# A planner that counts a pause between dependent VectorE instructions, with its due dates searched anew, in a one-core attention and scan kernel

## The chip, the cores and the metric

The kernel runs on one core of a Trainium2 chip. The metric is the device time of one execution in microseconds (us), as the median of several runs. The engines are named as the profile names them: PE is TensorE (PEld its weight loads), DVE is VectorE, ACT is ScalarE, POOL is GpSimd, SP is SyncE, which issues the DMAs.

## What is computed

All in fp32, for 4096 rows of x and 3202 rows of context, both 512 wide, with 8 heads of 64:

```python
x = layernorm(builder_state, g1, beta1); base_n = layernorm(base_state, g1, beta1)
q = heads(x, Wq, bq); k = heads(base_n, Wk, bk); v = heads(base_n, Wv, bv)
attn = softmax(einsum('bhqd,bhkd->bhqk', q, k) / sqrt(64))
x = builder_state + (attn @ v).reshape(...) @ W_o.T + b_o
U = (layernorm(x, g2, beta2) @ W_in.T + b_in) @ Bmat
def step(s, u_t):                      # 4096 steps over the rows, 64 states, from zero
    s = silu(s @ A.T) + u_t
    return s, s
out = x + states @ Cmat + (program_probs.mean(1) @ W_prog.T + b_prog)
```

## The kernel before

**The work and its tiles.** A first plan prepares K and V. The main plan, with which this case deals, runs over 64 *units*. A unit is a block Q of 512 queries (8 of them), a pair hp of heads (4) and a half of 256 queries (2); in the first seven blocks unit i has Q = i div 8, hp = (i div 2) mod 4, half = i mod 2. A unit goes through 13 steps c over the keys. In step c PE computes `scores` (L1131, 16 quarter-array matmuls of 64x64 weights into one of two PSUM score banks, ring "s"), ACT the exponential `weights` (L1209, tile p), PE the `product` with V (L1267, into the PSUM pair po0 and po1, ring "o", of which there is one), and DVE adds the weights up over the steps (`add`, L1217, each add taking the result of the one before it: tile acc). At the last step the product also takes in the keys that are left over (L1255).

**The end of a unit.** `output` (ACT, L1317) copies po0 out and `join` (DVE, L1321) adds po1 to the copy. Only then may the next unit's product 0 write the pair. `rest` (DVE, L1202) adds the left-over keys' weights to acc, `fold` (DVE, L1224) adds acc's halves, `swap` (ACT, L1236) copies its partition halves across, `gather` (DVE, L1241) adds that copy, `sums` (PE, L1295) adds over the partitions, `den` (ACT, L1339) takes the sums out, `inverse` (DVE, L1344) and `scale` divide the output by them. `sums` needs both slots of the PSUM ring "m". For every second unit these hold first the sample from which the exponent's shift comes: `sample` (PE, L1151), `maximum` (DVE, L1165), `spread` (PE, L1173), `base` (DVE, L1186 to L1187), and `extra` (ACT, L1193), whose reading frees the slots.

**What runs beside it.** For each block Q the plan also makes the next block's queries and finishes a block before it: `outs` (PE, L391, tiles pax and pay, full-array matmuls through `by_sevenths`, with its reads on DVE at L1664 and `so` at L1646), the row's statistics (DVE L1402, POOL L1406 to L1408), its scaling (ACT, L1414), the flip by 32x32 blocks (DVE, L468), `mod` (POOL, L1710), and the SP transfers. Scans of the 64 states run beside the last units: chain a (PE L1919, ACT, DVE L1954) and chain b; behind the last unit stands a chain l of 20 dependent steps (its rows are normalized into xh_yl, L2105, and turned on PE, L332), then its products (L1993) and outputs.

**What sets the order.** Each engine's order is decided ahead of time by the class `Plan`. A piece has an engine, a cost in ns, the pieces that it comes after, a due date, and ring slots that it takes and gives. `Plan.order` runs a simulated clock: an engine that is free takes, of the pieces that are ready and whose slots are free, the one with the earliest due date. The table `SHIFT` moves the due date of all pieces of one name by a number of STEPs of 2150 ns. A successor on another engine becomes ready `LATE` after the piece's simulated end (150 ns after DVE, 110 after ACT, 250 after PE); a successor on the same engine became ready at the simulated end itself. `OVER` lets the next instruction of DVE start 80 ns ahead of the end of the one before, if it does not depend on it. PE pays 200 and 280 ns for going between quarter-array and full-array matmuls. The order that comes out is the program; on the chip each engine runs its list strictly in that order and waits on semaphores. So costs and dates of the planner cost no time themselves: only the order counts.

```python
heapq.heappush(events, (free[e], -1, p["at"], p))                    # L195: engine free
heapq.heappush(events, (now + cost, 0, p["at"], p))                  # L196: same engine's successors
heapq.heappush(events, (now + cost + self.LATE[e], 1, p["at"], p))   # L197: other engines' successors
```

Of the kernel before, what the change touches and what calls it, by code (L numbers as in the profile page):

```python
# [75 lines left out]
class Plan:  # L76
# [8 lines left out]
    OVER = {"DVE": 80, "ACT": 100}  # L85
    ENTER, LEAVE = 200, 280
# [6 lines left out]
        "row.store": -0.5, "fold": 17, "rows.outs": 8.25, "heads": -12, "spread": 1.75, "query.flip": -11,  # L93
        "states": -4.5, "inverse": 14.75, "extra": 10, "scale": -51.75, "rest": 11, "row.mod": -20,
        "joined0": -10.25, "b": 1, "add.l": -23, "l.stats": -34.75, "last": -4.5, "base": -34.75,
        "inverse.l": -35, "rows.inputs": 5, "maximum": -13.5, "fall": -19, "query.stats": -10, "den": 4.5,
        "row.scaled": 16, "l.h": -11, "row.stats": -21.25, "rows.turn": 11, "query.scaled": 7.5, "l.mod": 7.5,
        "close": -10, "swap": 5.75, "products": -8, "gather.l": -8, "l.ys": -10, "fall.l": -2, "weights": -3.5,
        "rows.s": 2, "l.x1": 1, "l.kept": 8, "tq": 20, "l.store": -2, "row.move3": 9, "l.from": -5,
        "l.copy": -12, "l.states": -8, "l.turn": -4, "row.flip": 3.5, "swap.l": -18, "l.near": 4,  # L100
        "differ": -0.25, "row.load": 12, "add": -6, "rest.l": -8, "den.l": 11.5, "query.factors": 16,
        "sevenths": -6, "l.z": -2, "gather": 1, "scale.l": -0.5, "outs": 1, "output": -12, "query.move3": 3,
        "number": 0.25, "l.inputs": -4, "q": -12, "sums": -4, "row.move2": 10, "row.move1": -0.25,
        "query.move0": -0.5, "stored1": -12, "counted": 1, "to": 12, "sums.l": 9, "row.kept": 8, "so": 11.75,
        "stored0": 2, "l.scaled": -0.25, "row.move0": 4, "rise": -1, "join": -12, "sample": 2.5,
        "l.idle": -0.25, "risen": -0.5, "c2": 0.5, "yb": 2, "query.load": 8,
# [23 lines left out]
    def order(self):  # L130
# [29 lines left out]
        while len(out) < len(pieces):  # L160
            for e in self.LATE:
# [15 lines left out]
                p = best[1]  # L177
# [18 lines left out]
                heapq.heappush(events, (now + cost, 0, p["at"], p))  # L196
# [23 lines left out]
def xattn_ssm_kernel(  # L220
# [1206 lines left out]
    def queries(plan, Q, d):  # L1427
# [4 lines left out]
        for half in range(2):  # L1432
# [171 lines left out]
    def project_by_sevenths(plan, Q, d, index):  # L1604
# [16 lines left out]
        for half in range(2):  # L1621
            for t in range(2):
                k = kss[half][t]
                first = (*kss[half][0], "load")
                plan.add((*k, "load"), "SP", 800, partial(load, half, t),
                         [first] if t else [from_(d - 6 * STEP)], d - 6 * STEP + 2 * half + t, [] if t else ["x"])
                plan.add((*k, "row"), "POOL", 1270, partial(row, half, t),
                         [(*k, "load"), from_(d - 2 * STEP)], d - STEP)
# [134 lines left out]
    def project(plan, Q, halves, d, index):  # L1763

        for half in halves:
# [41 lines left out]
            for t in range(2):  # L1807
                plan.add((*ks[t], "load"), "SP", 800, partial(load, t),
# [727 lines left out]
    with tc.manual_schedule():  # L2536
# [8 lines left out]
            Plan.OVER,  # L2545
        )
# [109 lines left out]
```

## Time and profile before

| | us |
|---|---|
| median of 3 runs (lowest, highest) | 1921.72 (1920.82, 1922.46) |
| the profiled execution | 1921.14 |
| its span in the trace | 1919.4 |
| PE busy | 1892.6 (99%) |
| PEld busy | 1375.6 (72%) |
| DVE busy | 1557.7 (81%) |
| ACT busy | 1174.9 (61%) |
| POOL busy | 253.5 (13%) |

The mean granted TensorE clock was 0.996 of full speed. A row of the timeline gives the start of an instruction in us from the start of the span, how long it took, its engine and line, the tiles written and read, its size, how many like it stand one behind the other (xN), and in brackets how long the engine was idle before it and whose result came last. Matmuls overlap, so the time of a set of 16 is longer than the distance to the next set. In group rows and waits the last numbers are the busy or waiting time, the count, and the mean or longest.

### The profile page before, as it was taken

To read this page: it belongs to the slowest core of one execution; us is meant where nothing else is said; L and a number is where in the kernel's file an instruction comes from. 1 tells how busy PE (TensorE), PEld (TensorE's weight loads), DVE (VectorE), ACT (ScalarE), POOL (GpSimd) and SP (SyncE) were. 2 spreads that over 40 slices of the span, in tenths; PEclk is the share of its full clock that TensorE was granted. 3 is DMA by queue.
4 is the path that set the end of the run, shared out by engine and by line. 5 is a ranking of instruction groups with operands and counts; after the bars stand their busy time and mean duration, and the time that the engine had idled before them with its cause. 6 is when DMAs were issued, how large, how long until landed. Compare 5 with 4: busy or idle time off the path is not lost.

```text
span 1919.4 us, 68812 instructions
## 1 busy us (share of the span) xinstructions
PE 1892.6 (99%) x29632; PEld 1375.6 (72%) x29632; DVE 1557.7 (81%) x2133; ACT 1174.9 (61%) x1675; POOL 253.5 (13%) x386
## 2 busy tenths in 40 slices
PE   9999999999999999999999999999999999999997
PEld 5887677777677767776777777776777677777664
DVE  6642799788979898798978897989879897989675
ACT  3242677575756576657757575657665775756642
POOL 6120300012001210021001200021002100120114
PEclk9999999999999999999999999999999999999998
DMA  8654233133323342323413332334232431545475
GB/s 253 164 150 123 58 102 89 45 104 91 101 63 106 91 114 82 94 70 108 109 42 108 85 106 65 104 93 112 83 91 64 117 107 42 174 119 165 139 205 189
DMA packets 260769, 207.55 MB, mean 108 GB/s; under 512 B 94633, under 2 KB 233897, under 8 KB 260461
## 3 DMA queue, kind: packets, MB, share of 16 engines
q1 hardware_dynamic: 256440, 196.48, 35.7%
q10 hardware_dynamic: 4020, 6.62, 1.2%
q8 instruction: 235, 3.85, 0.8%
q14 instruction: 74, 0.60, 0.1%
HBM read 156.32 MB, written 29.88 MB: 97 GB/s over the span
## 4 chain that ended last, share of the span: by engine, by line


## 5 line engine op out<-in xcount | busy, mean ns | idle before, releaser
L1209 ACT ACTIVATE p<-s,shifts 128x1024 f32<-128x1024 f32 (+1 forms) x832 | 891.9, 1081 | 448.5 <-PE s L1131 422.5
L1217 DVE TENSOR_TENSOR acc<-p,acc 128x1024 f32<-128x1024 f32 (+1 forms) x704 | 841.4, 1195 | 111.2 <-ACT p L1209 81.7
L1131 PE MATMUL s<-q,k 64*64 64x256 f32 x12800 | 859.6, 377 | 3.8 <-ACT p L1209 3.7
L1267 PE MATMUL po<-p,v 64*64 64x256 f32 x12800 | 860.3, 376 | 2.0 <-DVE o L1321 2.0
L1131 PEld LDWEIGHTS s<-q,k 64*64 64x64 f32 x12800 | 501.4, 133 | 211.4 <-ACT p L1209 23.1
L1267 PEld LDWEIGHTS po<-p,v 64*64 64x64 f32 x12800 | 505.3, 133 | 180.3 <-DVE o L1321 6.0
L1619 POOL TENSOR_TENSOR xr<-xr,rowb 128x512 f32<-128x512 f32 x28 | 35.7, 1274 | 850.5 <-DVE acc L1217 739.1
L1344 DVE RECIPROCAL rd<-rd 128x256 f32<-128x256 f32 (+1 forms) x64 | 110.0, 1718 | 6.4 <-ACT rd L1339 6.4
L1217 DVE TENSOR_TENSOR acc<-p,p 128x1024 f32<-128x1024 f32 x64 | 78.3, 1224 | 21.0 <-ACT p L1209 21.0
L1710 POOL TENSOR_TENSOR xr<-x,modb 128x512 f32<-128x512 f32 x28 | 40.9, 1470 | 309.1 <-DVE x L1664 174.9
L1236 ACT COPY swap<-acc 64x256 f32<-64x256 f32 x126 | 50.9, 404 | 18.1 <-DVE acc L1224 15.4
L1241 DVE TENSOR_TENSOR acc<-swap,acc 64x256 f32<-64x256 f32 x126 | 52.3, 415 | 6.7 <-ACT swap L1236 5.1
L1202 DVE TENSOR_TENSOR acc<-x,acc 2x256 f32<-2x256 f32 x128 | 54.9, 429 | 1.5
L1556 ACT ACTIVATE q<-qx,bias 128x256 f32<-128x256 f32 x42 | 17.6, 470 | 56.9 <-PE qx L391 56.9
L569 DVE TENSOR_TENSOR ks<-pky,ks 128x512 f32<-128x512 f32 x15 | 10.4, 692 | 43.6 <-PE pky L391 28.7
L1224 DVE TENSOR_TENSOR acc<-acc 128x512 f32<-128x512 f32 x63 | 43.2, 686 | 0.8
L563 ACT ACTIVATE ks<-pkx,bias 128x256 f32<-128x256 f32 x40 | 16.8, 470 | 44.1 <-PE pkx L391 32.6
L1321 DVE TENSOR_TENSOR o<-po,o 128x256 f32<-128x256 f32 x64 | 26.9, 420 | 11.4 <-ACT o L1317 11.0
L1193 ACT ACTIVATE x<-sm,shifts 128x256 f32<-128x256 f32 x64 | 26.8, 472 | 14.7 <-DVE shifts L1187 14.1
L1406 POOL TENSOR_SCALAR rstd_x<-mv_x 128x1 f32<-128x1 f32 x28 | 12.2, 434 | 175.7 <-DVE mv_x L1403 174.0
L1165 DVE TENSOR_REDUCE m<-sm 128x1 f32<-128x256 f32 x64 | 24.0, 417 | 12.0 <-PE sm L1151 12.0
L1339 ACT ACTIVATE rd<-pd 128x128 f32<-128x128 f32 x126 | 33.2, 271 | 0.4 <-PE pd L1295 0.4
(307 smaller groups left out, 1762.9 us busy)
## 6 DMA issues: line engine op xcount, KB each, us to landing
k<-kd SPq DMA_DIRECT2D x432, 128.0 KB, 2.3
v<-vd SPq DMA_DIRECT2D x432, 128.0 KB, 2.3
xn<-x SPq DMA_DIRECT2D x448, 32.0 KB, 1.9
xr<-in_x_dram SPq DMA_DIRECT2D x30, 256.0 KB, 3.6
x1d<-xr SPq DMA_DIRECT2D x30, 256.0 KB, 2.1
x<-in_x_dram SPq DMA_DIRECT2D x28, 256.0 KB, 3.3
cx<-in_ctx_dram SPq DMA_DIRECT2D x25, 256.0 KB, 4.6
kd<-ks SPq DMA_DIRECT2D x20, 256.0 KB, 2.3
```

Of the source, the lines that this page charges most:

```text
L1131: nc.tensor.matmul(s[k0 : k0 + HD, a, b, :], kts[(*w["at"][:2], c)][r, b * CK + k0 : b * CK + k0 + HD], q[r], start=True, stop=True, skip_ ...
L1202: made = nc.vector.tensor_tensor(to[r], t[r], to[r], ALU.add)
L1209: nc.scalar.activation(t[:, :, :nb, :], w["ps"][c][:, :, :nb, :], AF.Exp, bias=w["shift"])
L1217: return nc.vector.tensor_tensor(w["acc"][:, :, :nb, :], t[:, :, :nb, :], before[:, :, :nb, :], ALU.add)
L1224: return nc.vector.tensor_tensor(acc[:, :, 0, :], acc[:, :, 0, :], acc[:, :, 1, :], ALU.add)
L1236: nc.scalar.copy(w["swap"][r], of[(1 - k) * HD : (2 - k) * HD])
L1241: made = nc.vector.tensor_tensor(of[r], w["swap"][r], of[r], ALU.add)
L1267: nc.tensor.matmul(w["po"][k][a * HD : (a + 1) * HD, :QU], vts[Q, hp, c][r, b, a * HD : (a + 1) * HD], t[r, a, b, :], start=(c == 0 and b ...
L1339: nc.scalar.activation(to, of, AF.Copy, accum_out=rises[:, 3 * i + k : 3 * i + k + 1])
L1344: nc.vector.reciprocal(w["rd"][:, part], (w["pd"] if last else w["rd"])[:, part])
L1619: return nc.gpsimd.tensor_tensor(xs[half][:, t], xs[half][:, t], rowb, ALU.add)
L1710: return nc.gpsimd.tensor_tensor(xt[:, t], x1[:, t], modb, ALU.add)
```

## The change

The planner gets a new number, 100 ns for DVE: a piece on DVE that takes the result of another DVE piece becomes ready that much after it. The main plan alone is given it; the first plan keeps its order. SP's cost for issuing a load of x is 500 instead of 800 ns in three places. Some 25 entries of `SHIFT` have other values; those which the prediction speaks of are swap 5.75 to -2.25, gather 1 to 0, sums unchanged, den 4.5 to 6.5, rows.outs 8.25 to 10.25, outs 1 to -3, scale -51.75 to -55.75. No instruction computes anything else than before, and no wait is written by hand; the lists of the engines hold the same pieces in another order. The lines of the changed kernel stand 1 or 2 further down.

```diff
+    SELF = {"DVE": 100}
...
-        "row.store": -0.5, "fold": 17, "rows.outs": 8.25, "heads": -12, "spread": 1.75, "query.flip": -11,
+        "row.store": -0.5, "fold": 17, "rows.outs": 10.25, "heads": -12, "spread": 1.75, "query.flip": -11,
...
-    def __init__(self, rings, held, over={}):
-        self.over = over
+    def __init__(self, rings, held, over={}, own={}):
+        self.over, self.own = over, own
...
-                heapq.heappush(events, (now + cost, 0, p["at"], p))
+                heapq.heappush(events, (now + cost + self.own.get(e, 0), 0, p["at"], p))
...
-                plan.add((*ks[t], "load"), "SP", 800, partial(load, t),
+                plan.add((*ks[t], "load"), "SP", 500, partial(load, t),
...
             Plan.OVER,
+            Plan.SELF,
```

ACT's list at the boundary of units 10 and 11 (Q 1, hp 1, half 0 and then 1; tile names carry Q, hp, half and, for p and s, the step). Before, the swap of unit 10 stands behind the second weights of unit 11:

```order
L1209 ACTIVATE p_1_1_1_0_5417<-s_1_1_1_0_5398,shifts_74 128x1024
L1209 ACTIVATE p_1_1_1_1_5438<-s_1_1_1_1_5419,shifts_74 128x1024
L1236 COPY swap_1_1_0_5450<-acc_1_1_0_5155 64x256 x2
L1209 ACTIVATE p_1_1_1_2_5461<-s_1_1_1_2_5440,shifts_74 128x1024
L1209 ACTIVATE p_1_1_1_3_5485<-s_1_1_1_3_5467,shifts_74 128x1024
L1317 COPY o_1_0_0_4723<-po0_1_1_0_5207 128x256
```

The same engine and place after the change (the first two weights of unit 11 read as before):

```order
L1210 ACTIVATE p_1_1_1_2_5460<-s_1_1_1_2_5440,shifts_74 128x1024
L1210 ACTIVATE p_1_1_1_3_5483<-s_1_1_1_3_5464,shifts_74 128x1024
L1318 COPY o_1_0_0_4721<-po0_1_1_0_5207 128x256
L1210 ACTIVATE p_1_1_1_4_5511<-s_1_1_1_4_5488,shifts_74 128x1024
L1210 ACTIVATE p_1_1_1_5_5529<-s_1_1_1_5_5502,shifts_74 128x1024
L1194 ACTIVATE x_1_2_0_5543<-sm_1_2_0_0_5199,shifts_74 128x256
L1194 ACTIVATE x_1_2_0_5543<-sm_1_2_0_1_5200,shifts_74 128x256
L1210 ACTIVATE p_1_1_1_6_5572<-s_1_1_1_6_5548,shifts_74 128x1024
L1340 ACTIVATE rd_1_0_1_5588,rises_90<-pd_1_0_1_0_5558 128x2x64
L1237 COPY swap_1_1_0_5590<-acc_1_1_0_5165 64x256 x2
```

The swap has moved behind the weights of step 6 and between the two copies of `den` of the unit before; `output` (o_1_0_0) now follows the weights of step 3 with no swap among them.

DVE's list at the same place. Before, from the ninth add of unit 10, fold and the first add of unit 11 follow the last add, then come two flips (L468), `gather` (L1241), `join` (L1321) and `rest` (L1202):

```order
L1217 TENSOR_TENSOR acc_1_1_0_5155<-p_1_1_0_9_5328,acc_1_1_0_5155 128x1024
L1217 TENSOR_TENSOR acc_1_1_0_5155<-p_1_1_0_10_5352,acc_1_1_0_5155 128x1024
L1217 TENSOR_TENSOR acc_1_1_0_5155<-p_1_1_0_11_5372,acc_1_1_0_5155 128x1024
L1217 TENSOR_TENSOR acc_1_1_0_5155<-p_1_1_0_12_5396,acc_1_1_0_5155 128x2x256
L1224 TENSOR_TENSOR acc_1_1_0_5155<-acc_1_1_0_5155 128x2x256
L1217 TENSOR_TENSOR acc_1_1_1_5463<-p_1_1_1_1_5438,p_1_1_1_0_5417 128x1024
L468 STREAM_TRANSPOSE x1_256_4978<-xh_y256_5384 128x16x32
L468 STREAM_TRANSPOSE x1_256_4978<-xh_y384_5385 128x16x32
L1241 TENSOR_TENSOR acc_1_1_0_5155<-swap_1_1_0_5450,acc_1_1_0_5155 64x2x128 x2
L1321 TENSOR_TENSOR o_1_0_0_4723<-po1_1_1_0_5208,o_1_0_0_4723 128x256
L1202 TENSOR_TENSOR acc_1_1_1_5463<-x_1_1_0_4784,acc_1_1_1_5463 2x2x128 x2
```

After, from the same add:

```order
L1218 TENSOR_TENSOR acc_1_1_0_5165<-p_1_1_0_9_5327,acc_1_1_0_5165 128x1024
L469 STREAM_TRANSPOSE x1_256_4965<-xh_y256_5383 128x16x32
L1218 TENSOR_TENSOR acc_1_1_0_5165<-p_1_1_0_10_5351,acc_1_1_0_5165 128x1024
L469 STREAM_TRANSPOSE x1_256_4965<-xh_y384_5384 128x16x32
L1218 TENSOR_TENSOR acc_1_1_0_5165<-p_1_1_0_11_5372,acc_1_1_0_5165 128x1024
L1218 TENSOR_TENSOR acc_1_1_1_5473<-p_1_1_1_1_5438,p_1_1_1_0_5416 128x1024
L1218 TENSOR_TENSOR acc_1_1_0_5165<-p_1_1_0_12_5395,acc_1_1_0_5165 128x2x256
L1203 TENSOR_TENSOR acc_1_1_1_5473<-x_1_1_0_4773,acc_1_1_1_5473 2x2x128 x2
L1322 TENSOR_TENSOR o_1_0_0_4721<-po1_1_1_0_5208,o_1_0_0_4721 128x256
L1218 TENSOR_TENSOR acc_1_1_1_5473<-p_1_1_1_2_5460,acc_1_1_1_5473 128x1024
```

The two flips now stand between dependent adds of unit 10, `rest` and `join` follow its last add, and fold and gather have moved behind the join.

PE's list in unit 9 (Q 1, hp 0, half 1), where the `sums` of unit 7 stand (tiles pd). Before, they follow product 2:

```order
L1267 MATMUL po1_1_0_1_4750<-p_1_0_1_2_4683,v_1_0_0_2_4197 64x256
L1295 MATMUL pd_0_3_1_0_4800<-acc_0_3_1_4022,ones_70 64x128
L1295 MATMUL pd_0_3_1_1_4801<-acc_0_3_1_4022,ones_70 64x128
L1295 MATMUL pd_0_3_1_0_4800<-acc_0_3_1_4022,ones_70 64x128
L1295 MATMUL pd_0_3_1_1_4801<-acc_0_3_1_4022,ones_70 64x128
L1131 MATMUL s_1_0_1_7_4810<-q_1_0_3728,k_1_0_0_7_4222 64x256 x8
```

After, they follow the scores of step 6 and stand ahead of product 2:

```order
L1132 MATMUL s_1_0_1_6_4778<-q_1_0_3728,k_1_0_0_6_4195 64x256 x8
L1296 MATMUL pd_0_3_1_0_4789<-acc_0_3_1_4022,ones_70 64x128
L1296 MATMUL pd_0_3_1_1_4790<-acc_0_3_1_4022,ones_70 64x128
L1296 MATMUL pd_0_3_1_0_4789<-acc_0_3_1_4022,ones_70 64x128
L1296 MATMUL pd_0_3_1_1_4790<-acc_0_3_1_4022,ones_70 64x128
L1268 MATMUL po0_1_0_1_4752<-p_1_0_1_2_4683,v_1_0_0_2_4197 64x256
```

The sums have moved one product ahead.

More of the change, by code (lines that the diff above doesn't have):

```diff
@@ L92 @@
     SHIFT = {
-        "row.store": -0.5, "fold": 17, "rows.outs": 8.25, "heads": -12, "spread": 1.75, "query.flip": -11,
[L94 to L106, printed above, removed]
-    }
-    def __init__(self, rings, held, over={}):
-        self.over = over
+        "row.store": -0.5, "fold": 17, "rows.outs": 10.25, "heads": -12, "spread": 1.75, "query.flip": -11,
@@ new lines @@
+        "rows.s": 2, "l.x1": 1, "l.kept": 6, "tq": 20, "l.store": -2, "row.move3": 11, "l.from": -5,
+        "l.copy": -12, "l.states": -8, "l.turn": -4, "row.flip": 3.75, "swap.l": -18, "l.near": 4,
+        "differ": 12.25, "row.load": 12, "add": -6, "rest.l": -8, "den.l": 11.5, "query.factors": 16,
+        "sevenths": -6, "l.z": -2, "scale.l": -0.5, "outs": -3, "output": -12, "query.move3": 3, "number": 0.25,
+        "l.inputs": -4, "q": -12, "sums": -4, "row.move2": 2, "row.move1": -0.25, "query.move0": 1.5,
```

12 lines of the change are left out of this document (10 added, 2 removed).

## The prediction, made before the changed kernel had run

> **What bounds the kernel now.** I read the page first, then the waits, then the timeline at the waits, and last the order of the two kernels.
>
> ```profile
> PE 1892.6 (99%) x29632; PEld 1375.6 (72%) x29632; DVE 1557.7 (81%) x2133; ACT 1174.9 (61%) x1675; POOL 253.5 (13%) x386
> L1209 ACT ACTIVATE p<-s,shifts 128x1024 f32<-128x1024 f32 (+1 forms) x832 | 891.9, 1081 | 448.5 <-PE s L1131 422.5
> L1217 DVE TENSOR_TENSOR acc<-p,acc 128x1024 f32<-128x1024 f32 (+1 forms) x704 | 841.4, 1195 | 111.2 <-ACT p L1209 81.7
> ```
>
> PE is busy for 99% of the span, and the others idle mostly because of it (ACT's 448.5 us ahead of the weights, 422.5 of them for PE's scores). PE's work is the same after the change, so only PE's own waits, and the distances that they stretch, can be won or lost. Undisturbed, the sets of 16 matmuls start 705.61 - 704.75 = 0.86 us apart:
>
> ```profile
> 704.75 1.04 PE L1267 MATMUL po<-p,v 64*64 64x256 f32 x16
> 705.61 1.04 PE L1131 MATMUL s<-q,k 64*64 64x256 f32 x16
> ```
>
> PE's waits, each row with its sum, count and longest:
>
> ```profile
> PE s L1131 <- ACT p L1209: 3.7, 11, 0.7
> PE po L1267 <- DVE o L1321: 2.0, 7, 0.9
> PE za L1919 <- DVE scan L1954: 1.4, 2, 1.1
> PE tp_yl L332 <- DVE xh_yl L2105: 1.5, 1, 1.5
> ```
>
> The first two rows are small in sum, but they come as a pair at six places, one in each block (units 10, 18, 26, 34, 42, 50). There they cost more than the brackets say, since a wait also empties the overlap of matmuls. The sum below is made against the profiled execution (1921.14); the median of the runs lies 0.58 above it.
>
> **Term 1: the swap among the weights (gain).** The boundary of units 10 and 11, from the timeline:
>
> ```profile
> 475.31 1.22 DVE L1217 TENSOR_TENSOR acc<-p,p 128x1024 f32<-128x1024 f32 x1
> ...
> 475.43 0.83 ACT L1236 COPY swap<-acc 64x256 f32<-64x256 f32 x2 [1.21 <-DVE acc L1224]
> ...
> 476.48 0.61 PE L1267 MATMUL po<-p,v 64*64 64x256 f32 x8
> 477.45 2.10 PE L1131 MATMUL s<-q,k 64*64 64x256 f32 x32 [0.36 <-ACT p L1209]
> 477.70 1.30 DVE L468 STREAM_TRANSPOSE x<-xh_y 128x512 f32<-128x512 f32 x2 [1.16 <-POOL xr L1710]
> ...
> 479.78 0.42 DVE L1321 TENSOR_TENSOR o<-po,o 128x256 f32<-128x256 f32 x1
> 480.13 0.83 DVE L1202 TENSOR_TENSOR acc<-x,acc 2x256 f32<-2x256 f32 x2
> 480.26 1.74 PE L1267 MATMUL po<-p,v 64*64 64x256 f32 x27 [0.18 <-DVE o L1321]
> ...
> 481.63 0.38 PE L1131 MATMUL s<-q,k 64*64 64x256 f32 x1
> ```
>
> ACT stands still for 1.21 us at the swap, which waits for DVE's fold, with the weights of steps 2 and 3 and `output` queued behind it. So PE's scores wait for a weights (0.36), and then the product for the join (0.18). An undisturbed boundary, where the swap stands behind `output`:
>
> ```profile
> 627.31 0.61 PE L1267 MATMUL po<-p,v 64*64 64x256 f32 x8
> ...
> 629.58 1.91 PE L1267 MATMUL po<-p,v 64*64 64x256 f32 x32
> ...
> 631.31 1.04 PE L1131 MATMUL s<-q,k 64*64 64x256 f32 x16
> ```
>
> From the half set of products to the next scores but one: 481.63 - 476.48 = 5.15 here, 631.31 - 627.31 = 4.00 there, so 1.15 lost. Four others are alike by their brackets (the list above has seven waits for the join, 2.0 us in all with one of 0.9, which leaves 1.1, six of 0.18). One is worse, 1107.00 - 1101.49 = 5.51, that is 1.51 lost:
>
> ```profile
> 1101.49 0.61 PE L1267 MATMUL po<-p,v 64*64 64x256 f32 x8
> ...
> 1107.00 0.38 PE L1131 MATMUL s<-q,k 64*64 64x256 f32 x1
> ```
>
> After the change the swap stands behind the weights of step 6, and nothing on ACT waits for the fold there. The six sites give 5 x 1.15 + 1.51 = **7.26 us**, if the join is in time. What is late next is the join itself: DVE has to do the last adds of the unit, now with two flips among them, `rest` and `join` before product 0 of the next unit. I followed DVE's new list at unit 18 with these rows:
>
> ```profile
> 670.59 12.66 DVE L1217 TENSOR_TENSOR acc<-p,acc 128x1024 f32<-128x1024 f32 x10
> ...
> 679.23 0.80 ACT L1414 ACTIVATE xh_y<-x,nm_y,rstd_y 128x512 f32<-128x512 f32 x1
> ...
> 685.06 0.61 PE L1267 MATMUL po<-p,v 64*64 64x256 f32 x8
> ```
>
> Ten adds in a row, nine full and one half, take 12.66 us (about 1.33 a full one, though one lasts 1.20 by its group) and end at 683.25. With two flips more among them (1.30), the first add of unit 19 (1.22), `rest` (0.83) and `join` (0.42) that is 687.0. Product 0 is due 629.58 - 627.31 = 2.27 after the half set, at 687.33. The second flip needs ACT's scaling, which ends at 680.03, ahead of its turn. Of the 0.3 us between, the pauses of dependent instructions take some; I estimate 0.15 of slack. So I take the whole gain, and hold its return as a rival.
>
> [...]
>
> **Term 2: sums one product earlier (loss).** In units 9, 17, 25, 33, 41 and 49 the sums of the unit two before now stand ahead of product 2. They need the slots that ACT's `extra` frees:
>
> ```profile
> 631.60 0.84 ACT L1193 ACTIVATE x<-sm,shifts 128x256 f32<-128x256 f32 x2
> 632.17 1.04 PE L1267 MATMUL po<-p,v 64*64 64x256 f32 x16
> 633.03 0.40 PE L1295 MATMUL pd<-acc,ones 64*64 64x128 f32 x8
> ```
>
> `extra` ends at 631.60 + 0.84 = 632.44. PE now asks for the slots at 632.17 instead of 633.03, and must wait 0.27 us and a semaphore's way. I take 0.4, so 6 x 0.4 = **2.4**; the ends are 0 (an earlier `extra`, since the swap ahead of it has gone behind) and 0.46 each.
>
> **Term 3: den and swap ahead of weights 2 (loss).** At the boundary of units 9 and 10, a copy of `den` and the swap now stand ahead of the weights of step 2 of the next unit. Weights 2 come 0.6 to 0.8 later, against this room:
>
> ```profile
> 664.88 0.42 DVE L1321 TENSOR_TENSOR o<-po,o 128x256 f32<-128x256 f32 x1
> ...
> 665.41 1.91 PE L1267 MATMUL po<-p,v 64*64 64x256 f32 x32
> ```
>
> The join ends at 665.30, 0.11 ahead of the product. It comes about as late as that, so 0.1 at six places, **0.6**; ends 0 and 0.2 each.
>
> **Term 4: changes between quarter and full arrays.** The new list has 103 of them, the old 101. One shows as 640.27 - 639.30 = 0.97 against 0.86:
>
> ```profile
> 639.30 1.04 PE L1267 MATMUL po<-p,v 64*64 64x256 f32 x16
> 640.27 1.99 PE L391 MATMUL pax<-wo,o 128*128 128x256 f32 x8
> ```
>
> Two more at 0.1 are **0.2**.
>
> **Term 5: scores in a row (gain).** With two score banks, a third set of scores in a row waits for ACT:
>
> ```profile
> 1753.34 1.09 PE L1131 MATMUL s<-q,k 64*64 64x256 f32 x16 [0.30 <-ACT p L1209]
> 1754.62 1.09 PE L1131 MATMUL s<-q,k 64*64 64x256 f32 x16 [0.19 <-ACT p L1209]
> ```
>
> These lie 1.28 apart, 0.42 over the 0.86, and twice that is 0.85. The new list puts products 0 and 1 of unit 60 between them. Of the 3.7 us of such waits the six sites have about 5 x 0.36 + 0.73 = 2.5, these two 0.5, and the other three, 0.7, lie in the first block, whose order changed at the same kind of place. I take 0.85 + 0.7 = **1.5 gained**, ends 0 and 2.
>
> **Term 6: the matmuls of outs for block 6, about 8 us earlier (loss).** Their DVE reads fall among adds; one that stands behind an add is up to 1.2 late. I take **0.5**, ends 0 and 1.2.
>
> **Term 7: chain a beside the last units (gain).** Its two waits are the 1.4 in the list above. Each step of the chain now stands with more of PE's work ahead of it. I take half, **0.7**; ends 0 and 1.4.
>
> **Term 8: behind the last unit.** The matmuls that turn the last rows wait 1.5 us for DVE. The new list has a step of chain b, the products of group 0 and another step ahead of them, about 1.1 us of PE work that no longer comes later. Against that, DVE does the last unit's add 12 later, and the rows it normalizes come later. Behind them stand the 20 steps of chain l, whose work doesn't change:
>
> ```profile
> 1875.39 1.04 PE L1919 MATMUL zl<-scan,a_t 64*64 64x128 f32 x16
> ```
>
> Its first step stays within about 0.1 us of 1875.39 by my reading. I take **0.5 gained**; ends 1.5 gained and 1.9 lost.
>
> SP's smaller cost for the loads of x moves issues of 17 pieces by a place or so. SP is hidden behind transfers that have microseconds to spare; at nothing, since no wait of PE in the list names a DMA.
>
> Sum: -7.26 + 2.4 + 0.6 + 0.2 - 1.5 + 0.5 - 0.7 - 0.5 = -6.26. 1921.14 - 6.26 = 1914.9 for a profiled execution, and with the 0.58 **1915.5 us** for the median.
>
> **The rivals.** *The gain comes back in part.* For it: the six joins have little to spare, and all ends of the losses together (2.8 + 1.2 + 0.2 + 1.2 + 1.9 = 7.3, no gain but term 1) just undo the 7.26. Against it: several would have to fall ill. That gives up to 1921.7, within 0.2% of no change (a difference of 3.84 us, about what a measurement of this kernel can tell from none).
>
> *Slower: DVE's order holds the join.* In the new list two flips stand ahead of `rest` and `join`, and each waits for ACT's scaling of a row half; a late scaling holds all that is behind it on DVE, while before the flips stood behind the last add. It can hold: the flips of unit 10 waited 1.16 us for POOL. With the join x us later than I have it, product 0 waits x - 0.15, at six places. From x = 1.2 the 6.26 are gone (6 x 1.05 = 6.3). At x = 1.9 the sum is -6.26 + 6 x 1.75 = +4.2: 1925.9 for the median. For it: DVE is the second busiest engine (81%), and such a wait for one thing held another in the old kernel (the 1.21 of the swap). Against it: the scaling is over 7 us ahead of the join.
>
> *More gain.* Terms 2, 3 and 6 at nothing, 7 and 8 at their full ends: -7.26 + 0.2 - 1.5 - 1.4 - 1.5 = -11.5, so 1910.2.
>
> *The planner's numbers don't bind.* If the joins were held by something else than ACT's order, the time would stay at 1921.7. Against it: the bracket at the swap names the fold.
>
> **How the numbers follow.** The forecast has 0.52, more gain 0.08, gain returned 0.20, not binding 0.05, DVE's order 0.15. Of the last a third is still within 0.2%. So faster by over 0.2% (under 1917.9) has 0.60, within 0.2% 0.30, slower (over 1925.6) 0.10. The range goes from 1910 (all gains) to 1923.5: it takes in gain returned and part of DVE's order, and leaves out about 0.15. The likeliest case alone has 1911 to 1918.
>
> **What would show it.** Right: at the six sites no bracket ahead of the scores and the join, 4.0 us where 5.15 were, ACT's swap without a wait; the waits for p and for o down by about 4 us in sum; a new wait of some 0.3 at L1296 for `extra`. Wrong: a bracket at the product that names the join (L1322) at units 18, 26 and so on, flips on DVE with idle time before them, or a chain l that starts later against its last product.

## The result, and the profile after

The changed kernel takes 1905.8 us, the median of 4 runs (1904.57 to 1906.81). The kernel before, run beside it, takes 1922.09 (1920.82 to 1922.7). The ratio is 0.9916, with a 95% interval of 0.9899 to 0.9933. So it is 16.3 us faster, where 6.3 were predicted, and below the predicted range. The profiled execution took 1904.96, and its span fell from 1919.36 to 1903.09 (16.27).

Of the page: the span, the engines, and the group rows of the products and the scores.

```profile
span 1903.1 us, 68781 instructions
PE 1886.3 (99%) x29632; PEld 1382.5 (73%) x29632; DVE 1547.7 (81%) x2133; ACT 1176.0 (62%) x1675; POOL 254.6 (13%) x386
L1268 PE MATMUL po<-p,v 64*64 64x256 f32 x12800 | 851.2, 377 | 1.3 <-DVE o L1322 0.9
L1132 PE MATMUL s<-q,k 64*64 64x256 f32 x12800 | 851.9, 377 | 0.3 <-ACT p L1210 0.2
```

The scores' waits for ACT are nearly gone: 0.3 us of idle time in all, 0.2 of it for ACT, where the list of waits had 3.7. Of the products' seven waits for the join (2.0) one is left, the 0.9 in the first 240 us, which was there before. The site of term 1 now, from the timeline:

```profile
476.00 0.61 PE L1268 MATMUL po<-p,v 64*64 64x256 f32 x8
...
476.43 1.91 PE L1132 MATMUL s<-q,k 64*64 64x256 f32 x32
...
477.44 0.42 DVE L1322 TENSOR_TENSOR o<-po,o 128x256 f32<-128x256 f32 x1 [0.32 <-ACT o L1318]
...
478.27 1.91 PE L1268 MATMUL po<-p,v 64*64 64x256 f32 x32
...
480.00 1.04 PE L1132 MATMUL s<-q,k 64*64 64x256 f32 x16
...
482.57 0.83 ACT L1237 COPY swap<-acc 64x256 f32<-64x256 f32 x2
```

From the half set to the next scores it is 480.00 - 476.00 = 4.00, as forecast, with no bracket on PE. The join ends at 477.86, 0.4 ahead of its product, and the swap waits for nothing. The site of term 2, in unit 9:

```profile
421.64 1.04 PE L1132 MATMUL s<-q,k 64*64 64x256 f32 x16
422.19 0.83 ACT L1194 ACTIVATE x<-sm,shifts 128x256 f32<-128x256 f32 x2
422.71 0.19 PEld L1296 LDWEIGHTS pd<-acc,ones 64*64 64x64 f32 x2 [0.48 <-ACT x L1194]
```

The sums' weights wait 0.48 for `extra`, a wait that the prediction forecast, at 0.3 to 0.4.

To see where the 16.27 us came from, I took in both traces the start of the left-over products (L1255, after L1256) of each unit as a landmark, and asked by how much the changed kernel is ahead at each. A step is by how much this lead grows from one landmark to the next.

| steps | predicted gain | measured |
|---|---|---|
| to unit 8 (first block; term 5 in part) | 0.7 | 1.09 |
| 8 to 9 and its like, six (terms 2, 3) | -3.0 | 6 x -0.62 = -3.7 |
| 10 to 11 and its like, six (term 1) | 7.26 | 5 x 1.55 + 1.91 = 9.7 |
| all others from unit 9 to 56 (term 4) | -0.2 | 1.8 |
| 56 to 63 (terms 5 in part, 6, 7) | 1.05 | 1.4 |
| behind the landmark of unit 63 (term 8) | 0.5 | 62.74 - 56.82 = 5.9 |
| sum | 6.3 | 16.3 |

Of the missing 10 us 5.4 lie behind the last unit. There the granted clock tells the two kernels apart. The view of windows: length, busy time of PE, PEld, DVE, ACT and POOL with counts, PEclk, DMA share, GB/s. Before, two neighbouring stretches of 3.41 us at the first turns of the last rows, and two at the last steps of the chains:

```profile
1868.31:1871.72 3.41, 1.72 (x13) 1.17 (x14) 2.49 (x5) 0.80 (x3) 3.15 (x4) 1.00 0.34 103
1871.72:1875.13 3.41, 3.41 (x26) 2.96 (x27) 1.13 (x4) 0.65 (x2) 1.11 (x2) 0.50 0.33 125
...
1892.20:1895.61 3.41, 1.17 (x18) 0.60 (x12) 1.65 (x7) 1.15 (x5) 1.68 (x2) 1.00 0.94 320
1895.61:1899.02 3.41, 3.35 (x36) 2.81 (x36) 1.21 (x5) 0.96 (x3) 0.91 (x2) 0.50 0.34 104
```

After, the stretches with the same work:

```profile
1860.27:1862.27 2.00, 1.20 (x12) 0.83 (x8) 2.00 (x3) 1.27 (x3) 2.00 (x2) 1.00 0.01 4
1862.27:1864.27 2.00, 1.93 (x23) 1.52 (x21) 0.74 (x4) 0.80 (x2) 2.00 (x4) 1.00 0.87 329
...
1886.27:1888.27 2.00, 2.00 (x44) 1.36 (x36) 1.72 (x5) 1.09 (x4) 0.82 (x2) 1.00 0.87 290
```

In the kernel before, PE is granted half its clock from 1871.72 to 1875.13 and from 1895.61 to 1899.02, each time behind a stretch in which it was busy for 1.72 or 1.17 of 3.41 us. Each costs, by my estimate, at most 3.41 x 0.5 = 1.7 us of PE's work. The sixteen 128x128 matmuls of L2121, which start from 1871.6 to 1873.9, last 421 ns in the median; the same ones (L2122) last 272 in the changed kernel, at full clock. After, the clock is full until 1897.91, in the last output's add. What PE waited for ahead of the first drop and ahead of the second in the kernel before:

```profile
1869.01 0.66 PE L332 MATMUL tp_yl<-ident,xh_yl 128*128 128x128 f32 x4 [1.47 <-DVE xh_yl L2105]
1869.59 0.44 PE L1919 MATMUL z<-scan,a_t 64*64 64x128 f32 x4
1871.02 0.63 PE L2111 MATMUL py_o<-ident,xh_yl 128*128 128x128 f32 x4 [0.99 <-DVE xh_yl L2105]
...
1894.47 0.43 PE L1919 MATMUL z<-scan,a_t 64*64 64x128 f32 x4 [1.54 <-DVE scan L1954]
```

The prediction quoted the 1.47 as a wait worth 1.1 us of work, not as the cause of a slower clock behind it.

### The profile page after: what moved, and what is told of

Same layout as the page of the kernel before. It is cut to its first block, busy times and chain, and to the rows that moved or that the text cites. A ratio compares the mean times of both kernels' runs of the same rounds, so it can differ in the third digit from the quotient of the medians.

```text
span 1903.1 us, 68781 instructions
## 1 busy us (share of the span) xinstructions
PE 1886.3 (99%) x29632; PEld 1382.5 (73%) x29632; DVE 1547.7 (81%) x2133; ACT 1176.0 (62%) x1675; POOL 254.6 (13%) x386
## 4 chain that ended last, share of the span: by engine, by line
## 5 line engine op out<-in xcount | busy, mean ns | idle before, releaser
L1268 PE MATMUL po<-p,v 64*64 64x256 f32 x12800 | 851.2, 377 | 1.3 <-DVE o L1322 0.9
L1711 POOL TENSOR_TENSOR xr<-x,modb 128x512 f32<-128x512 f32 x28 | 35.5, 1276 | 197.5 <-DVE acc L1218 155.5
L1407 POOL TENSOR_SCALAR rstd_x<-mv_x 128x1 f32<-128x1 f32 x28 | 18.9, 676 | 269.7 <-DVE mv_x L1404 268.0
L570 DVE TENSOR_TENSOR ks<-pky,ks 128x512 f32<-128x512 f32 x15 | 10.4, 692 | 43.6 <-PE pky L392 28.7
L1415 ACT ACTIVATE xh_y<-x,nm_y,rstd_y 128x512 f32<-128x512 f32 x30 | 24.2, 808 | 13.0 <-POOL nm_y L1409 13.0
```

The source lines that it names most:

```text
L1268: nc.tensor.matmul(w["po"][k][a * HD : (a + 1) * HD, :QU], vts[Q, hp, c][r, b, a * HD : (a + 1) * HD], t[r, a, b, :], start=(c == 0 and b ...
L1711: return nc.gpsimd.tensor_tensor(xt[:, t], x1[:, t], modb, ALU.add)
```

## The experiments

`behind_(a, b)` moves a piece directly behind another in its engine's list; the other lists stay. Times are medians, ratios are to the kernel before, run beside it. By "xr_l" I mean the start of the first add (L2214) that makes the last output rows, at the end of chain l's work.

**1. The smaller SP cost alone** (before with it).

```diff
-                plan.add((*ks[t], "load"), "SP", 800, partial(load, t),
+                plan.add((*ks[t], "load"), "SP", 500, partial(load, t),
```

> The kernel before, with one part of the change alone: SP's cost for the loads of x is 500 instead of 800. In the planned order this moves six sums (units 7, 15, 23, 31, 39, 47) ahead of product 2 of the unit two later, as the whole change does, a few row statistics on DVE by one add, and a few pieces of block 6. Theory A (the sums wait for extra's slots wherever they stand there): each of the six places loses about 0.4 us, with a wait at the sums that names extra; the profile's distance from the last product of unit 8 to that of unit 9 grows by 0.4 and the time by 2 to 3 us, to about 1924.5. Theory B (as the prediction had it for SP's cost: nothing): the time stays within 0.5 us of the kernel before.

1921.21, ratio 1.0004 (0.9994 to 1.0013): the time does not tell it from the kernel before. The trace does: the step 8 to 9 is 0.36 longer at all six blocks, and most of it comes back later in each block, so that 0.6 us net are lost at unit 63. So the smaller cost by itself puts the sums ahead of product 2: not "at nothing", if small.

**2. Only the swap and the gather moved, at the six sites** (before with them).

```diff
+        for i in range(10, 51, 8):
+            behind_(("swap", i), ("output", i))
+            behind_(("gather", i), ("rest", i + 1))
```

> The kernel before, with one move alone at the six sites (units 10, 18, 26, 34, 42, 50): ACT's swap stands directly behind output instead of ahead of the weights of step 2, and DVE's gather behind rest instead of ahead of join. Theory A (ACT's wait for the fold is all that the site loses): the six places give 1.3 us each, 7.9 in all, 1914. Theory B (behind the swap the next thing in the way is DVE: the two flips that wait for POOL's mod still stand ahead of join): the flips end about 2.5 us after the last half set begins as before, so the join is late by some 0.7 us still, each site gives 0.4 to 0.7 and the sum is 2.5 to 4 us, 1918 to 1919.5, with a wait of product 0 that names the join and is longer than 0.18.

1920.3, ratio 0.9998 (0.9988 to 1.0008). No gain. The scores no longer wait, and the site's step gains 0.32, but the steps behind it lose as much again, since the join still holds the product. The timeline:

```profile
477.66 1.30 DVE L468 STREAM_TRANSPOSE x<-xh_y 128x512 f32<-128x512 f32 x2 [1.17 <-POOL xr L1710]
...
478.89 0.39 DVE L1321 TENSOR_TENSOR o<-po,o 128x256 f32<-128x256 f32 x1
479.33 1.28 PEld L1267 LDWEIGHTS po<-p,v 64*64 64x64 f32 x27 [0.48 <-DVE o L1321]
```

The join (478.89, before 479.78) still stands behind two flips that wait for POOL, and the product's weights wait for it. So term 1 is not the swap's place alone.

**3. The six sites as a whole** (before with the changed order of ACT, DVE and POOL there: the swap behind `den`, flips among the adds, `rest` and `join` behind add 12, fold and gather behind the join).

```diff
+            behind_((*r, 2, "flip"), ("add", i, 9))
+            behind_((*r, 3, "flip"), ("add", i, 10))
...
+            behind_(("join", i), ("rest", i + 1))
...
+            behind_(("fold", i), ("add", i + 1, 3))
+            behind_(("gather", i), ("add", i + 1, 5))
+            behind_(("swap", i), ("den", i - 1, 0))
```

> The kernel before, with the order of the changed kernel at the six sites alone (units 10, 18, 26, 34, 42, 50), on ACT, DVE and POOL: flips among the last adds, rest and join and base ahead of fold and gather, swap between the two copies of den, POOL's last mod not held for the fold. Theory A (ACT's queue and DVE's queue hold the site together, and the swap alone could give nothing since join, base and with it extra and sums were late in its place): no wait of PE for weights or join is left at the sites, each gives 1.3 to 1.6 us, 8 to 9.5 in all, 1912. Theory B (the gain of the changed kernel at these places comes from what else moved in the blocks, the row statistics and inputs): less than 3 us.

1910.62 (4 runs), ratio 0.9948 (0.9934 to 0.9963): 10.4 us. The steps are +1.55, 1.55, 1.55, 1.91, 1.56 and 1.55, as in the changed kernel. This is all of term 1.

**4. The swap put back** (changed kernel; fold directly behind the last add, swap behind the weights of step 1).

```diff
+        for i in range(10, 51, 8):
+            behind_(("fold", i), ("add", i, 12))
+            behind_(("swap", i), ("weights", i + 1, 1))
```

> The changed kernel, with two moves undone at the six sites: DVE's fold stands directly behind the unit's last add, and ACT's swap behind the weights of step 1 of the next unit, where the kernel before had it. Theory A (the swap that waits for the fold holds weights, scores and join): PE's waits for weights come back at six places, 1 to 1.6 us each, and the time is 6 to 9.5 us over the changed kernel's 1905.8, 1912 to 1915. Theory B (with the flips out of the way DVE comes to the fold early enough): at most 2 us over.

1931.62 (4 runs), ratio 1.0052 (1.0038 to 1.0067): 10.6 us slower than the kernel before, and 4.5 per site in the trace against the changed one, more than Theory A said. The timeline and the windows of one site:

```profile
476.98 0.82 ACT L1237 COPY swap<-acc 64x256 f32<-64x256 f32 x2 [3.38 <-DVE acc L1225]
...
478.99 3.12 PE L1132 MATMUL s<-q,k 64*64 64x256 f32 x32 [2.51 <-ACT p L1210]
```

```profile
476.23:479.64 3.41, 0.90 (x20) 0.51 (x16) 1.43 (x3) 2.62 (x4) 0.00 (x0) 1.00 0.13 38
479.64:483.05 3.41, 3.41 (x46) 2.10 (x40) 2.21 (x6) 2.51 (x4) 0.00 (x0) 0.50 0.13 38
```

With flips and an add ahead of it, the fold now comes later than it did before, the weights wait behind the swap for 3.38 us, and PE for 2.51. And behind that wait the clock falls to half at each of the six sites (the mean is 0.993, in the changed kernel 0.999): up to 1.7 of the 4.5.

**5. The sums behind product 2 again** (changed kernel).

```diff
+        for i in range(7, 48, 8):
+            behind_(("sums", i), ("product", i + 2, 2))
```

> The changed kernel, with the six sums (units 7, 15, 23, 31, 39, 47) moved back behind product 2 of the unit two later, where the kernel before had them. Nothing else moves. Theory A (they wait there for the slots that extra frees, 0.36 to 0.42 us each): the step from unit 8 to unit 9 and the five like it are 0.4 us shorter, the time 2.2 to 2.5 us below the changed kernel's 1905.8, about 1903.4. Theory B (the loss of 0.62 us in this step comes from the matmuls of outs that stand after scores now): less than 0.5 us.

1902.42 (5 runs), ratio 0.9909 (0.9896 to 0.9923). In the profile all six steps of -0.62 are gone, and the span is 1899.2, 3.9 below the changed kernel's. So what terms 2 and 3 forecast is one loss, all of it the sums'. This kernel has the shortest span of all, by 2 us; its median is the lowest too, though only 0.6 below run 6, and its runs spread over 3.7.

**6. The pause alone** (before with SELF and its use; dates and SP's cost for the loads of x as before). The run also raised SP's cost for two loads of the first plan from 500 to 800.

```diff
+    SELF = {"DVE": 100}
...
+                heapq.heappush(events, (now + cost + self.own.get(e, 0), 0, p["at"], p))
...
-                add(("c.load", c), "SP", 500, partial(load_chunk, c), [], u - 17000 - early, ["cx"])
+                add(("c.load", c), "SP", 800, partial(load_chunk, c), [], u - 17000 - early, ["cx"])
...
-            add(("a.load", at_), "SP", 500, partial(load, *steps[k]), stored,
+            add(("a.load", at_), "SP", 800, partial(load, *steps[k]), stored,
```

> The kernel before with the planner's 100 ns between dependent instructions on DVE alone: old dates, SP's cost 800. In the order output of the six sites follows the weights of step 3 without the swap, but the scaling of two row halves stands among them, the flips directly ahead of join, and the sums stand five products later. Theory A (the pause alone changes the order everywhere and is not worth anything without dates searched with it): between 3 us faster and 15 us slower than the kernel before. Theory B (the pause is the part that brings the gain at the six sites): 6 to 10 us faster, 1911 to 1915.

1903.05 (4 runs), ratio 0.9911 (0.9896 to 0.9926): 17 us, more than Theory B had. The first plan's costs moved a few pieces there, but they don't explain it: the first unit's landmark is at 224.17, in the kernel before at 224.35. The order is not that of the changed kernel (the sums stand five products later), so this is another way to the same gain. The new dates and SP's cost add nothing that can be measured on top.

**7. The dates without the pause** (changed kernel without SELF).

```diff
-            Plan.SELF,
```

> The changed kernel without the 100 ns that the planner counts between dependent instructions on DVE: new dates and SP's 500 alone. In the order the swap of the six sites stands between the weights of step 2 and output, and base ahead of join; sums 7 and so on stand as in the changed kernel; half of the moves behind the last unit are there. Theory A (the dates carry the gain only together with the pause): most of the gain is gone, 1914 to 1921, with waits for the join at the six sites. Theory B (the dates alone carry it): within 3 us of the changed kernel, 1905 to 1909.

1922.41, ratio 1.0004 (0.9995 to 1.0013). The body loses 5.25 us against the kernel before, and the part behind it gains 4.26. The dates, with SP's 500, bring no gain without the pause.

**8. Only the part behind the last unit** (before; the last 296 pieces, those behind the products of unit 63, stand in the changed kernel's order by a written list).

```diff
-        for piece in plan.order():
+        pieces_ = plan.order()
+        last_ = {p["name"]: p for p in pieces_[-len(tail):]}
+        pieces_[-len(tail):] = [last_[n] for n in tail]
+        for piece in pieces_:
```

> The kernel before up to the last product of unit 63, and from there on the order of the changed kernel for the 296 pieces that are left on all engines. Theory A (the order of these pieces carries the gain behind the last unit: chain b and the products of group 0 fill PE's waits, and the granted clock does not fall): from the last unit's left-over matmuls to the end of the span 57 us as in the changed kernel instead of 62.7, a gain of 5 to 6 us, 1916.5, granted clock 1.0 in every stretch of the tail. Theory B (the tail is shorter because the last units reach it in another state): less than 2 us of gain, and the clock falls to about 0.5 again in the tail.

1915.29, ratio 0.9971 (0.9961 to 0.998): 5.5 us. From the landmark to the end it is 56.58. With the sites' 10.4 that makes 15.9 of the change's 16.3.

**9 to 11. Idle matmuls in PE's waits of chain l** (before; `a_t` times itself into a bank that nobody reads). Run 9 puts 12, 8 and 10 ahead of the two turns and a late step of chain b, run 10 5, 3, 6 and 2, run 11 5 and 3 ahead of the turns only.

```diff
+        def idle_(n):
+            for k in range(n):
+                nc.tensor.matmul(sv["py"][1][k % 2][:, :P], a_t, a_t, start=True, stop=True)
...
+        fill = {("l.turn", 0): 5, ("l.turn", 1): 3}
```

> The kernel before with idle matmuls alone added, 128x128 at some 0.11 us each, whose results nobody reads: 12 ahead of the first turn of the last rows, 8 ahead of the second, 10 ahead of step 12 of chain b, that is in the three waits of PE of 1.47, 0.99 and 1.54 us. Nothing else moves. Theory A (these waits let the granted clock fall to half for about 3.5 us twice, in which PE's work takes 1.6 to 1.7 us longer each time, and the path runs through it): the clock stays at 1.0 and the time falls by 2 to 3.5 us, to about 1919. Theory B (the half clock is a sign of the waits, and its work is hidden or fills time that would be waited anyway): the time stays within 0.5 us, or rises by up to 1 us for the added work.

1922.74, ratio 1.0012 (1.0003 to 1.0022). Too many: each matmul shows as two of about 0.11 us, the first 12 as 24 that take 2.95 us, and they held the turns up by more than the clock was worth.

> The kernel before with idle matmuls added as in the run with 12, 8 and 10 of them, but shorter than the waits that they fill, since each of them showed as two of 0.11 us there: 5 ahead of the first turn of the last rows (1.1 us of the 1.47), 3 ahead of the second (0.66 of 0.99), 6 ahead of step 11 of chain b (1.3 of 1.54) and 2 ahead of its step 12 (0.44 of 0.65). Theory A (a wait costs its own length and, by the half clock that it brings, up to 1.7 us more): the granted clock stays at 1.0 behind the last unit in all executions, and the median falls to that of the executions before with a mean clock of 0.998, 1918 to 1918.5, by 2.5 us. Theory B (the half clock hides behind other waits): the time stays within 0.7 us.

22984.55 (6 runs). The third and fourth group wrote into the bank of chain b's steps, and the trace has 239650 instructions instead of 68812: most likely the values no longer converged and the kernel's own branch took it to its general path. This time says nothing. Up to there the clock was full (1.00 until 1891), and chain l's first step began 17.27 us behind the landmark, where the kernel before has 18.77.

> The kernel before with idle matmuls in the first two waits behind the last unit alone: 5 ahead of the first turn of the last rows and 3 ahead of the second, which leave most of 0.3 us of each wait. Theory A (the half clock after these waits is on the path): the first step of chain l starts 17.3 to 17.4 us after the left-over matmuls of the last unit instead of 18.8, in all executions, and the median falls by 1 to 1.5 us, the second fall of the clock left as it may be. Theory B (it is hidden): within 0.4 us.

1919.67, ratio 0.9998 (0.9989 to 1.0007). The first drop of the clock is gone and chain l's first step starts at +17.37; the second drop comes as before (the mean clock is 0.997, where the kernel before has 0.996). In the profile the part behind the landmark is 1.2 us shorter, as Theory A said; the medians don't resolve it.

**12. The last row earlier** (before; its products, copy and join moved ahead).

```diff
+        behind_(("products", 15, 0), ("l.idle", 17))
...
+        behind_(("copied", 15), ("differ", "b", 1))
...
```

> The kernel before, with the last rows' work alone moved to where the changed kernel has it: products of group 15 ahead of the last step of chain l on PE, their copy ahead of the last tanh on ACT, their join ahead of the last step on DVE. Theory A (the stores of these rows are issued together with the very last ones and prolong the transfers at the end): the time from chain l's end to the end of the span falls by 1.5 to 2.5 us, and the total by 1 to 2.5. Theory B (the end is set by the last store's own way): within 0.5 us, or up to 1 us longer, since chain l's last step is held by PE's products.

1920.06, ratio 0.9997 (0.9988 to 1.0006). From xr_l to the end 8.50, before 8.57. That is Theory B, though not the test it was meant to be: SP's list was not moved, and one store of that row still stood behind xr_l's.

**13 and 14. The changed order only up to chain l's terms, and only behind them** (before, with a list as in run 8). The lists around the terms, of run 13 and then of run 14:

```diff
+            ('l.kept', 0), ('products', 1, 0), ('stored1', 0), ('l.kept', 1), 'risen', ('products', 1, 1), 'l.terms',
...
+            ('l.kept', 1), ('products', 0, 0), 'risen', ('b', 'tanh', 2), 'l.terms', ('products', 0, 1),
```

> The kernel before, whose pieces behind the last unit stand in the changed kernel's order up to chain l's terms and in the old order behind them. Theory A (what the products of rows 0 and 1 ahead of chain l's terms buy is the clock: they fill TensorE's waits of 1.47 and 0.99 us, the half rate at 1872 to 1875 us does not come): the granted clock stays above 0.95 in the 4 us around chain l's terms, chain l's first step starts at most 17.8 us behind the landmark of the last unit though more work stands ahead of it (18.77 before), the last step of the rows is reached at about +52 (54.18 before), and the stores' end is as before (8.3 to 8.8 us from the last output's add to the end): 1 to 3 us less in the profile, a time of 1917.5 to 1919.5. Theory B (the gain lies in the order behind the terms): the clock may hold, yet the profile's part behind the last unit stays within 0.7 us of 62.74, and the time within 1 us of the kernel before.

1921.16, ratio 1.0001 (0.9992 to 1.001). The clock was held at the first turns (1.00 from 1868.59 to 1876.59), yet nothing was won: Theory A falls, and B, with the gain in the order behind the terms, has the time right. But the half clock had only moved: it came at the last steps, and for two stretches:

```profile
1890.97:1894.38 3.41, 1.76 (x32) 1.07 (x24) 2.01 (x6) 0.89 (x4) 1.71 (x3) 1.00 0.89 305
1894.38:1897.79 3.41, 2.76 (x33) 2.48 (x32) 0.84 (x5) 0.72 (x4) 0.75 (x2) 0.50 0.49 162
1897.79:1901.21 3.42, 3.42 (x42) 2.31 (x36) 2.25 (x5) 1.17 (x4) 2.18 (x3) 0.50 0.36 125
```

> The kernel before, whose pieces behind the last unit keep the old order up to chain l's terms and stand in the changed kernel's order behind them. Theory A: the half rate at the first turns comes as before where the profiled execution has it (chain l's first step at about +18.8), so 1.3 to 3 us of the changed kernel's 5.9 are missing; the second half rate at the last steps and the crowded stores are gone: from the last output's add to the end 6.0 to 6.4 us in place of 8.57, and the whole part 58.5 to 60 us; a time of 1917 to 1918.5. Theory B (all of it is the order behind the terms): 56.6 to 57.2 us, a time of 1915 to 1916.

1917.54, ratio 0.9984 (0.9975 to 0.9993), as Theory A said: the first drop is there (0.50 from 1871.24 to 1874.65), the second is not (1.00 from 1888.30 to 1898.53), from xr_l to the end it is 6.27, and the whole part takes 60.06.

**15. Without the last row's stores** (before; that row of the output is left out).

```diff
+            if j < 15:
```

> The kernel before without the two stores of the last row (that row of the output is left out). Theory A (in the kernel before three stores of 224 to 256 KB are issued within 0.6 us at the end and share the DMA engines, and the last one ends late for it; in the changed kernel the row's are over by then): from the last output's add to the end 6.0 to 6.4 us in place of 8.57, and nothing else moves: 2.3 us less, a time of 1917.5 to 1919. Theory B (the last store is as late by itself, and the changed kernel's end has another reason): 8.0 us or more, a time within 0.7 us of the kernel before.

1920.13, ratio 0.9999 (0.999 to 1.0008). From xr_l to the end 7.62: 0.95 of the 2.5 us between the two kernels is those stores, less than Theory A had, and the medians don't resolve it.

The runs together divide the part behind the last unit. The half-rate time is taken from the trace's clock records; what it costs at most is half of it.

| kernel | landmark to xr_l | at most lost to the half clock | difference | xr_l to the end |
|---|---|---|---|---|
| before | 54.18 | 3.41 | 50.8 | 8.57 |
| smaller SP cost (1) | 51.20 | 0 | 51.2 | 7.87 |
| swap and gather moved (2) | 51.21 | 0 | 51.2 | 8.33 |
| first turns filled (11) | 52.76 | 1.71 | 51.1 | 8.75 |
| changed order to the terms (13) | 54.46 | 3.41 | 51.1 | 8.41 |
| changed order behind them (14) | 53.80 | 1.71 | 52.1 | 6.27 |
| changed order of all (8) | 50.47 | 0 | 50.5 | 6.10 |
| changed kernel | 50.75 | 0 | 50.8 | 6.07 |

Runs 1 and 2 left the order behind the last unit as it was, and their profiled executions had no drop: the two drops of the kernel before cost 54.18 - 51.21 = 3.0 us against them, 3.4 at most. Without the clock's part the new order is worth nothing there (50.8 and 50.8) to 0.5 (50.75 against 51.2). The differences lie between 50.5 and 52.1, so less than about a us is not told apart by these single traces; the 52.1 of run 14 is not explained.

So the old order gets the drops or not, I take it, by where its waits fall: in run 2 the stretches that hold the waits have 1.91 us of PE's work or more, where the kernel before has 1.72 and 1.17, and the clock stays at 1.00. It differs from one execution to the next, too: of the 96 executions of the kernel before beside these runs, the 34 with a mean clock of 0.996 took 1921.6 in the median, the 51 with 0.997 1920.4 and the 11 with 0.998 1918.2. The 19 executions of the changed kernel and of runs 5 and 8, which have the changed order there, all have 0.999.

The 2.5 us between xr_l and the end lie on SP. Its last stores before and after:

```profile
1911.50 0.35 SPq L2218 DMA_DIRECT2D out_dram<-xr_l  x1
1911.97 0.36 SPq L2018 DMA_DIRECT2D out_dram<-row  x1
1912.10 0.37 ACTq L2218 DMA_DIRECT2D out_dram<-xr_l  x1
```

```profile
1897.73 0.33 SPq L2219 DMA_DIRECT2D out_dram<-xr_l  x1
1898.33 0.37 ACTq L2219 DMA_DIRECT2D out_dram<-xr_l  x1
```

SP then loads the convergence count and branches. In the trace's records of SP, the load ends 2.06 us behind ACT's last store before and 1.16 after; without the row's stores (15) it is 0.94. From the branch to SP's next instruction it is 2.83 before, 2.66 in run 15, 1.22 after and 0.47 in run 6. So 0.9 us belong to the row's store that stood behind xr_l's, and 1.6 to that branch. The other traces bear out the first: the load ends 2.02 to 2.20 behind ACT's store wherever such a store of a row stood behind xr_l's, and 0.91 to 1.18 where none did. The branch takes 1.97 to 3.03 in the eight traces with the old order at the end and 1.22 to 1.62 in the five with the changed one; what makes it long was not tried.

## Why the prediction was wrong, point by point

- **Term 8, the step that failed.** "I take **0.5 gained**; ends 1.5 gained and 1.9 lost" was a count of PE's work ahead of the turns and of chain l's steps, and as that it nearly holds: the order alone is worth 0 to 0.5. But it took the durations of the profiled execution as PE's own, though 6.8 us of them were at half clock, and it stopped at chain l. Measured were 5.9: 3.0 to 3.4 from the clock (runs 2, 11 and 13 show it come and go), the 0 to 0.5 of the order, and 2.5 behind xr_l, which the term did not look at. The rows that showed it were on hand. The first has PEclk 0.90 behind the last units (the changed kernel has 0.95 from 1850 on, all of that loss at its very end), where only the mean of 0.996 was read; the others stand in the list of PE's waits, where the prediction shows neither, though one is its second largest, and all of them lie behind the last unit:

```profile
1850.00:1920.00 70.00, 52.76 (x652) 34.33 (x644) 43.81 (x109) 19.14 (x62) 24.83 (x31) 0.90 0.67 201
```

```profile
PE z L1919 <- DVE scan L1954: 2.8, 4, 1.5
PE py_o L2111 <- DVE xh_yl L2105: 1.0, 1, 1.0
```

- **Term 1** was right in its mechanism and 2.4 too small. At "481.63" one score matmul starts, but three of the product stand at 481.83 (the prediction read a start as if the set ahead of it were over). Between landmarks the site is worth 1.55, not 1.15. Its joins were in time, with 0.4 to spare for the 0.15 estimated. Runs 2 and 3 add that it takes the flips' and the join's places on DVE, and not the swap's alone; term 1 put the whole 1.15 down to the swap, though it did follow the flips in the new list.
- **Terms 2 and 3** were forecast at 3.0 and measured at 3.7. Term 2's loss is 0.62 at each place, above its end of 0.46, and run 5 shows that all of it is the sums'; term 3's step, 9 to 10, is 0.00. That the two together came near is luck.
- **SP's cost "at nothing"** was the wrong reading of a list of waits: no wait named a DMA, but the number moves pieces of other engines. It moves the sums by itself (run 1).
- **Terms 4 to 7** came to 1.4 for the last units against 1.05, and 1.09 against 0.7 in the first block. The 1.8 us in small steps of 0.2 to 0.3 behind the sites were in no term. They show in part in runs 1 and 3; which entry makes them was not separated.
- **The rivals.** "More gain" had the direction and 0.08, but its end, 1910.2, was made from the terms' own ends and could not hold what no term had. "Gain returned" and "the planner's numbers don't bind" did not come: every site gained. The slower one (DVE's order holds the join) did not come; run 4 shows its price when the order is broken by hand. Its opposite, a plan without the pause (run 7), is no faster than before.
- **The pause.** The prediction left open how long it is. Its ten adds of 12.66 us answer that: the nine full ones last 1.225 in the trace and the half one 0.69, so (12.66 - 9 x 1.225 - 0.69) / 9 = 0.10 us lie between one and the next that takes its result, about the 100 ns that SELF plans. (The 1.20 "by its group" mixes full and half adds.) Run 6 has the worth of planning it: 17 us. Instructions that don't take each other's result overlap instead: behind one of 0.69 us the next starts after 647.64 - 647.04 = 0.60.

```profile
647.04 0.69 DVE L1646 TENSOR_TENSOR o<-o,o 128x512 f32<-128x512 f32 x1
647.64 0.68 DVE L1646 TENSOR_TENSOR o<-o,so 128x512 f32<-128x512 f32 x1
```

## What to carry to other kernels

Before costing an order from a trace, read the granted clock in windows of a few us around each wait of the busiest engine, at the ends of the program above all: a duration at half clock is not the work's own (421 ns here for a matmul that lasts 272 at full clock). Here waits of 1 to 1.5 us were followed by up to 1.7 us that the half clock cost, while the order that puts other work into them won 0 to 0.5 us besides. And a scheduler's number is judged by running it alone: here one number, the pause, gave the whole gain, and the others that came with it nothing that could be measured on top.

## What was not expected of the hardware

The two half-rate stretches of the clock last 3.41 us each (before) and begin 1895.61 - 1871.72 = 23.89 = 7 x 3.413 apart; in run 13 one begins at 1897.79, where another ends. The programs' ends and run 6 aside, those shown here followed stretches in which PE was busy for 0.90 (run 4) to 1.76 us (run 13). Stretches with 1.91 (run 2) and 1.99 (run 3) were followed by full clock; the last:

```profile
1881.61:1885.02 3.41, 1.99 (x32) 1.21 (x32) 2.19 (x6) 1.01 (x4) 2.01 (x3) 1.00 0.89 305
```

Run 6 does not fit a sharp bound: its half rate follows a stretch with 2.04 busy, and one with 1.74 was followed by full clock. And none of the stretches ahead of a drop was idle throughout: in the kernel before, two waits of 1.47 and 0.99 us, with 1.02 of work between them (1869.01 to 1870.03), stood ahead of the first.
